# A graph network's gated projection: bias sums, third parts and chunk weights moved around the seam of its first two quarters

## The chip, the cores and the metric

The kernel runs on one core of a Trainium2 chip. A core has five engines that run at the same time, each with its own instruction stream: TensorE (PE, matrix products; the weight loads before them are shown as PEld), VectorE (DVE), ScalarE (ACT), GpSimd (POOL) and SyncE (SP, whose queue issues most of the DMAs). They wait for each other through semaphores. The metric is the time of one execution in microseconds (us), as the median of repeated runs. A profile is one further execution recorded by the chip's hardware profiler.

## The reference

x holds 1024 nodes with 512 features, in 16 graphs of 64 nodes; every graph has a condition of 256 rows. The sizes that matter: D = 512, H = 8 heads of DH = 64, L = 4 layers, and a gated projection whose inner width is 4D = 2048.

```python
h = (x - mu) * rsqrt(var + EPS) * bn_w + bn_b
h = gcn(h, src, dst, gcn_in_w, gcn_in_b)            # sum over 16384 edges
for i in range(L):
    h = h + attn(ln(h, ln2_w[i], ln2_b[i]), cond, Wq[i], Wk[i], Wv[i], Wo[i])
    u = ln(h, ln3_w[i], ln3_b[i]) @ geglu_w[i] + geglu_b[i]      # 512 -> 4096
    val, gate = split(u, 2, axis=-1)                             # 2 x 2048
    f = val * gelu(gate)
    h = h + f @ ffo_w[i] + ffo_b[i]                              # 2048 -> 512
h = gcn(h, src, dst, gcn_out_w, gcn_out_b)
return x + (h + x_in)
```

The change lies in the last three lines of the loop, and in the last of the attention's stages before them.

## The kernel before

**Stages of a layer.** The attention goes over eight pairs of graphs, g = 0 to 7, 128 rows of h each (the tiles called hall in the profile). The gated projection has a value and a gate side of 2048 columns; it is worked in quarters of 512 columns, and a quarter in four pieces of 128, so sixteen pieces in all. The output product follows in units.

All large products are done with seven instead of eight block products (Strassen's way, in Winograd's form), so sums of blocks have to be made first: `sums_of_b` and `sums_of_a` (L229 to L242), `Chunk.sums` (L1086 to L1094).

**Quarter 0** is the class `Quad`, four of them, with plain f32 products (L297). Their first two products (`first`, `second`, tile ga) are interleaved with the end of the attention's last pair. There, the softmax of pair 7 is scaled (pr, L852, on VectorE), turned by TensorE (tr_pr), copied out of PSUM by VectorE and ScalarE in turn (pT, L884 and L886), and multiplied by the values (po, L870). `rest(fill)` does the other five products (tiles gb, gc, gd) with VectorE's additions between them and the activation by ScalarE (L1002). It calls `fill()` five times, and each call drives one step of a generator that prepares the next quarters, `all_parts`.

**Quarters 1 to 3** are twelve objects of class `Chunk`. Their f32 products are replaced by three fp32r products of parts: a high, a low and a third part of each operand. Of the right side (the LayerNorm's output, the same for all chunks) six of seven operands are split so, in the order `SPLIT = (0, 5, 6, 4, 1, 3)`: ScalarE makes the high part and a multiple of it, VectorE makes the third part (gr, L1044, `begin_right`) and the low part (gl, L1052, `finish_right`). Both are two VectorE operations of 128x512 for each operand, one for each half k. The left side is a chunk's weights. They are loaded by four DMAs on SP into gxa and gxb (L1084), summed by GpSimd (L1094) and split by `split_left`: high part by ScalarE (gha, ghb, L1057), low part by VectorE (gla, glb, L1058), third part by GpSimd (gsa, gsb, L1061).

A chunk is a flow of six steps, `steps`. `scale(i)` does the first two products of operand i and has ScalarE multiply the bank by 1 + TINY (L1124), `scale_onto(i)` lets VectorE do it and add a term (L1128), and `end(i)` adds the third product. The flows of two chunks overlap: while one starts, the one before it ends. Its results fT are stored to a DRAM buffer (f_dram, L1194) and fetched again by the output units (fr). These need parts as well: ah_f, al_f and as_f of fr (L314 to L317) and bh, bl and bs of the output weights wff (`split_w`, L1229 to L1236). Some of the latter are made early by the generator `output.ahead()`, in steps placed by the table `splits`.

**What sets the order.** A scheduler orders instructions by costs and due times, but whatever is wrapped in `pin` keeps the order of the program text on its engine; nearly all of the seam is pinned. `issue_after` and `waiting_for` add dependencies by hand. Tiles come from pools of fixed size, so a tile that is asked for waits until an earlier one of its ring has been read: `t512` (ten of 128x512), `slot` (36 of 128x1024) and `acc_tile`. SP issues DMAs in the order of the text, and a DMA that waits holds those behind it.

**The places that are touched** (lines of the kernel before): the loop over pairs, where `ln3_sums(nc.gpsimd, nb)` sums the LayerNorm's blocks on GpSimd; `add_bias` (L1532), which adds the output's bias to a tile of hall on GpSimd, eight times behind the last LayerNorm sums; `all_parts`; the loop over the quads, with the loads and splits of the first two chunks in it; the loop over the chunks; and the table `beside` of work for the next layer during the output units.

Of the kernel before, what the change touches and what calls it, by code (L numbers as in the profile page):

```python
# [11 lines left out]
F32R = mybir.dt.float32r  # L12
# [13 lines left out]
def gnn_kernel(  # L26
# [1010 lines left out]
    def begin_right(name, x, h, s):  # L1037

        nc.scalar.mul(h.bitcast(F32R), x, INWARD / TINY)
        for k in range(2):  # L1040
# [3 lines left out]
            pin(nc.vector.scalar_tensor_tensor(s.bitcast(F32R)[:, k, :], x[:, k, :], 1.0 / TINY,  # L1044
                                               more, OP.mult, OP.subtract))

    def finish_right(name, x, h):

        low = slot(name)
        for k in range(2):  # L1050
            yield low
            pin(nc.vector.scalar_tensor_tensor(low.bitcast(F32R)[:, k, :], x[:, k, :], 1.0 / TINY,  # L1052
                                               h[:, k, :], OP.mult, OP.subtract))
# [390 lines left out]
    for l in range(L):  # L1444
# [80 lines left out]
        def ln3_sums(t, nb):  # L1525

            c0 = nb % 4 * P
            of = [ln3T[i][k][:, :, c0:c0 + P] for k in range(2) for i in range(2)]
            return sums_of_b(t, *of, *(x[:, :, c0:c0 + P] for x in ln3S), nc.gpsimd)
# [36 lines left out]
        for g in range(NG - 1):  # L1566
            if g == NG - 2:
                take_ln3()
                raw = load_geglu(l, 0)
            probs = scores(l, g, qT, kTs.pop(g))  # L1570
            for end in ends:
                end()
            if g == NG - 2:
                with waiting_for(scores.last, mybir.EngineType.Pool):
                    left = geglu_weights(l, 0, *raw)
            if not g:
                with waiting_for(scores.last, mybir.EngineType.Pool):
                    wo7 = wo_sums(wo)
            if g in (1, 2):
                fetch_x(2 * l + g - 1)  # L1580
            k = keys(l, g + 1, wk, 1 if l == 0 and g == 0 else 0)
            for i, u in enumerate(k):
                u.begin()
                if i > 1:
                    k[i - 2].end()
            k[-2].end()
            v = values(l, g + 1, wv)
            oTs.append(mix(l, g, probs, vs.pop(g), (k[-1].end, nothing, v[0].begin)))
            if g == NG - 2:
                ln3_norm(g - 2, g - 1, behind=mix.last)  # L1590
            if g in (1, 2):
                base_of(2 * l + g - 1)
            if l == 0:
                fetch_cond(g + 3)
            if g % 2:
                blocks = pair_sums(l, g - 1, oTs)
                oTs.clear()
            with tc.issue_after(pair_sums.last.ins) if g % 2 else nullcontext():
                split_cond(l, g + 2)
            if l:  # L1600
                load_cond(l, g + 3)
            v[1].begin()
            v[0].end()
            v[2].begin()
            v[1].end()
            if g % 2:
                pair = attn_out_pair(g - 1, *blocks, wo7, bank(f"oab_{l}_{g}"), bank(f"ocd_{l}_{g}"),
                                     pin)
                next(pair)
                if g > 1:  # L1610
                    moments_into(mv_kept[:, 2 * (g - 3):2 * (g - 1)], [h[g - 3], h[g - 2]],
                                 f"ln3_{l}_{g - 3}")
            if g == NG - 2:
                for nb in range(4):
                    ln3_turn(nb, each=pin)
            v[3].begin()
            if g % 2:
                next(pair)
            v[2].end()
            ends = [v[3].end]  # L1620
            if g % 2:
                next(pair)
                ends.insert(0, lambda pair=pair: next(pair, None))
                if g == NG - 3:
                    scale_kept()
            if g == NG - 2:
                for nb in range(4, 6):
                    ln3_turn(nb, each=pin)
                for nb in (g - 2, g - 1):
                    ln3_sums(nc.gpsimd, nb)  # L1630
            if l == 0 and g + 3 < NG:
                turn_cond(g + 3, each=pin)
        oT, = oTs
# [17 lines left out]
        ln3_turn(g, (1, 1))  # L1651
        summed = ln3_sums(nc.vector, g)
        with tc.issue_after(summed.ins):
            for nb in range(NB):
                add_bias(nb)
        quads[2].second()
        quads[3].second()
# [10 lines left out]
        def finish_rights(*of):  # L1668
            for i in of:
                x, high, mid = begun[i]  # L1670
                flow = finish_right(f"gl_{l}_{i}", x, high)
                Chunk.rights[i] = high, next(flow), mid
                yield
                for _ in flow:
                    yield

        def all_parts():
            for i in SPLIT:
                yield from begin_right(f"gt_{l}_{i}", *begun[i])
                yield from finish_rights(i)  # L1680

        parts = all_parts()
        next(parts)
# [18 lines left out]

        for c, q in enumerate(quads):
            q.rest(fill)
            if c == 1:
                load()
                sum_chunk(0)
            if c == 2:
                split(0, False)
                split(0, True)  # L1710
        for _ in parts:
            pass
        load()
        sum_chunk(1)
        output = Output(l)
        ahead = output.ahead()
        fetches = [(R - 2, 0), (R - 2, 3), (R - 1, 1), (R - 1, 3)]
        splits = {(R - 2, 1): 3, (R - 2, 2): 2, (R - 1, 0): 3, (R - 1, 1): 2}
        before = None
        for r in range(1, R):  # L1720
            f = Gated(l, r)
            for c in range(KC):
                if (r, c) in fetches:
                    output.fetch_w(fetches.index((r, c)))
                if (r, c) == (R - 1, KC - 2):
                    output.fetch(0)
                chunk = ready.pop(0)
                flow = chunk.steps(lambda: sum_chunk(1))
                chunk.f = f
                next(flow)  # L1730
                split(0, False)
                load()
                for step in range(3):
                    if before:
                        next(before, None)
                    next(flow)
                    if step < splits.get((r, c), 0):
                        next(ahead)
                split(0, True)
                before = flow  # L1740
        output.split(0)
        output.fetch(1)
        for _ in range(3):
            next(before, None)

# [4 lines left out]
        if last:  # L1750
            hs_out.extend(RowsInTurn(f"hs_{n}_out") for n in ("high", "low"))

            def begin_last():
                for nb in (0, 1, 4, 5):
                    into_parts(nb)

            def fetch_counts():
                nonlocal again, dinv_row
                again, dinv_row = load_counts()

            def fetch_last():
                nonlocal w_out
                w_out = out_weights(nc.gpsimd, L, 0, load_w(gcn_out_w, "w_out"))

            beside = {8: begin_last, 9: fetch_counts, 13: fetch_last}
        else:
            half = [0, 1, 4, 5], [2, 3, 6, 7]
            wk, wv = [[], [], []], [[], [], []]

            def fetch_next():  # L1770
                nonlocal raw_wk
                raw_wk = load_w(Wk[l + 1], f"wk_{l + 1}")
                load_cond(l + 1, 0)

            def fetch_values():
                nonlocal raw_wv
                raw_wv = load_w(Wv[l + 1], f"wv_{l + 1}")

            def split_of(to, raw, name, i):
                for part, t in zip(to, right_parts(raw[i:i + 1], f"{name}_{l + 1}_{i}")):  # L1780
                    part.extend(t)

            def norm_first():
                take_moments(l + 1, half[0], 2)
                ready_first(l + 1, half[0])

            def fetch_more():
                nonlocal wq, ffb
                wq = load_w(Wq[l + 1], f"wq_{l + 1}")
                ffb = load_row(ffo_b, (l + 1) * D, f"ffb_{l + 1}")  # L1790
                load_cond(l + 1, 1)

            beside = {8: lambda: (fetch_next(), take_moments(l + 1, half[0], 0, 2)),
                      9: lambda: split_of(wk, raw_wk, "wk", 0),
                      10: lambda: split_of(wk, raw_wk, "wk", 1),
                      11: lambda: (norm_first(), fetch_values()),
                      12: lambda: split_cond(l + 1, 0),
                      13: lambda: split_of(wv, raw_wv, "wv", 0),
                      14: fetch_more}
        with in_order(mybir.EngineType.DVE):  # L1800
            for n in range(2 * UNITS):
                output.fetch(n + 2)
# [143 lines left out]
```

## Time and profile before

| | |
|---|---|
| time, median of 3 runs | 2390.27 us (2388.44 to 2392.40) |
| profiled execution | 2390.05 us, span 2388.3 us |
| mean granted TensorE clock | 0.994 |
| TensorE busy | 2324.4 us, 97% |
| VectorE busy | 1585.6 us, 66% |
| ScalarE busy | 1082.1 us, 45% |
| GpSimd busy | 794.7 us, 33% |

The span runs from the first to the last instruction; the execution's own time has what lies around it too. A row of the timeline gives the start (us from the span's start), the time that the group took, the engine, the line, the operation, what it writes and reads, its shape and count, and in brackets the idle time of its engine before it and who ended that. A row of busy time by windows gives the length, each engine's busy time and instruction count (PE, PEld, VectorE, ScalarE, GpSimd), the granted clock, the DMA share and GB/s. The four layers look alike; the rows that are shown are of the third (l = 2), which begins its gated projection at 1497.80.

### The profile page before, as it was taken

The numbers are of one execution on the slowest core, as the hardware profiler recorded it, in microseconds if no ns is written. First come the engines' busy times: TensorE is split into PE (matmuls) and PEld (weight loads), VectorE is DVE, ScalarE is ACT, GpSimd is POOL, SyncE is SP. The second block draws the span as 40 slices with busy tenths as digits, with TensorE's granted clock in tenths as the row PEclk, the third lists the DMA queues.
The fourth block names the chain that finished last, engine by engine and source line by source line (L and its number), as shares of the span: only waits on it lengthen the run. The fifth ranks groups of instructions, "written<-read, shape, count | busy, mean of one in ns | idle before, by whom it ended". The sixth has DMA issues, their size and how long they took to land. (4 is left out here: it accounts for less than half of the span.)

```text
span 2388.3 us, 33592 instructions
## 1 busy us (share of the span) xinstructions
PE 2324.4 (97%) x12272; PEld 1722.9 (72%) x12272; DVE 1585.6 (66%) x3024; ACT 1082.1 (45%) x2099; POOL 794.7 (33%) x731
## 2 busy tenths in 40 slices
PE   8999999899999999899999999989999999989999
PEld 5668886477867887477876888467786888557787
DVE  9874546777964445777984454867886554777864
ACT  7444454455344444454344444445334444445420
POOL 1142223563023224465022323466022224356211
PEclk9999999999999999999999999999999999999999
DMA  6052220235412110234522201134432111033550
GB/s 202 18 156 72 71 67 1 81 116 173 147 63 66 41 33 21 71 100 124 187 71 67 67 19 36 40 97 129 163 124 67 49 37 36 19 90 113 176 194 36
DMA packets 161068, 205.42 MB, mean 86 GB/s; under 512 B 11304, under 2 KB 101744, under 8 KB 160896
## 3 DMA queue, kind: packets, MB, share of 16 engines
q1 hardware_dynamic: 158800, 197.77, 26.0%
q0 software_dynamic: 1376, 4.30, 0.5%
q8 instruction: 102, 1.67, 0.3%
q10 hardware_dynamic: 720, 1.11, 0.1%
q14 instruction: 70, 0.57, 0.1%
HBM read 152.80 MB, written 50.34 MB: 85 GB/s over the span
## 5 line engine op out<-in xcount | busy, mean ns | idle before, releaser
L320 POOL TENSOR_TENSOR as_c<-ah_c,al_c 128x512 fp32r<-128x512 f32 x128 | 195.3, 1556 | 416.8 <-PE fy L1255 242.1
L1110 PE MATMUL g<-gr,gsa 128*128 128x512 f32 x384 | 142.0, 452 | 35.7 <-ACT g L1124 35.7
L377 ACT ACTIVATE v<-v 128x512 f32<-128x512 f32 x127 | 74.1, 583 | 220.5 <-PE v L366 218.4
L1061 POOL TENSOR_TENSOR gsa<-gha,gla 128x512 fp32r<-128x512 f32 x96 | 127.4, 1349 | 99.4 <-DVE gla L1058 99.4
L1255 PE MATMUL fx<-bs_wff,as_f 128*128 128x512 f32 x512 | 158.2, 390 | 2.0 <-DVE as_f L317 2.0
L1255 PE MATMUL fy<-bh_wff,ah_f 128*128 128x512 f32 x512 | 159.3, 392 | 0.0
L1255 PE MATMUL fy<-bl_wff,al_f 128*128 128x512 f32 x512 | 157.7, 389 | 0.0
L1124 ACT ACTIVATE g<-g 128x512 f32<-128x512 f32 x192 | 110.3, 581 | 99.3 <-PE g L1110 97.2
L314 ACT ACTIVATE ah_f<-fr 128x1024 fp32r<-128x1024 f32 x64 | 67.5, 1060 | 174.9 <-PE fy L1255 116.3
L366 PE MATMUL v<-bh_wv,ah_c 128*128 128x512 f32 x508 | 145.9, 409 | 0.0
L366 PE MATMUL v<-bs_wv,as_c 128*128 128x512 f32 x508 | 143.4, 404 | 0.0
L847 ACT ACTIVATE pr<-sc,nmax 128x256 f32<-128x256 f32 x256 | 118.3, 475 | 52.8 <-DVE nmax L842 52.1
L377 ACT ACTIVATE k<-k 128x512 f32<-128x512 f32 x125 | 72.7, 585 | 147.4 <-PE k L366 147.4
L366 PE MATMUL v<-bl_wv,al_c 128*128 128x512 f32 x508 | 136.4, 390 | 0.0
L366 PE MATMUL k<-ah_c,bh_wk 128*128 128x512 f32 x500 | 134.6, 391 | 0.0
L366 PE MATMUL k<-al_c,bl_wk 128*128 128x512 f32 x500 | 134.0, 390 | 0.0
L366 PE MATMUL k<-as_c,bs_wk 128*128 128x512 f32 x500 | 132.1, 395 | 0.0
L1137 ACT ACTIVATE g<-g,gcols 128x512 f32<-128x512 f32 x96 | 67.5, 704 | 132.4 <-DVE g L1145 129.9
L1110 PEld LDWEIGHTS g<-gr,gsa 128*128 128x128 f32 x384 | 72.4, 194 | 76.1 <-issue 61.8
L1110 PE MATMUL g<-gr,gha 128*128 128x512 f32 x384 | 121.0, 396 | 0.0
L1110 PE MATMUL g<-gl,gla 128*128 128x512 f32 x384 | 118.8, 390 | 0.0
L382 DVE COPY kT<-k 128x512 f32<-128x512 f32 x54 | 37.4, 692 | 118.4 <-PE k L366 118.4
(351 smaller groups left out, 5632.2 us busy)
## 6 DMA issues: line engine op xcount, KB each, us to landing
f_dram<-fT SPq DMA_DIRECT2D x128, 256.0 KB, 2.6
fr<-f_dram SPq DMA_DIRECT2D x64, 512.0 KB, 4.8
ct<-cond_dram SPq DMA_DIRECT2D x48, 512.0 KB, 4.4
wff<-in_L_gnn_ffo_w_dram SPq DMA_DIRECT2D x32, 512.0 KB, 4.8
gxb<-in_L_gnn_geglu_w_dram SPq DMA_DIRECT2D x96, 128.0 KB, 2.7
gxa<-in_L_gnn_geglu_w_dram SPq DMA_DIRECT2D x96, 128.0 KB, 2.8
cond<-in_L_gnn_cond_dram SPq DMA_DIRECT2D x32, 256.0 KB, 3.6
cond_dram<-ct SPq DMA_DIRECT2D x16, 512.0 KB, 4.0
```

Of the source, the lines that this page charges most:

```text
L314: nc.scalar.mul(twelve_bits(h), x, INWARD * TINY)
L320: nc.gpsimd.tensor_tensor(twelve_bits(s)[:, k, :], h[:, k, :], l[:, k, :], OP.subtract)
L366: pin(nc.tensor.matmul(self.bank, twelve_bits(left[k // 2])[:, k % 2, self.c * P:(self.c + 1) * P], twelve_bits(right[k // 2])[:, k % 2, : ...
L377: nc.scalar.mul(self.bank, self.bank, 1.0 + TINY)
L382: nc.vector.tensor_copy(self.to(), self.bank)
L847: nc.scalar.activation(pr3[:, a, :], ps3[:, a, :], AF.Exp, bias=nmax[:, a:a + 1], accum_out=tot[:, a:a + 1])
L1061: pin(nc.gpsimd.tensor_tensor(s_at, h_at, l_at, OP.subtract))
L1110: pin(nc.tensor.matmul(to, self.part(i, which)[:, k, :], self.rights[i][which].bitcast(F32R)[:, k, :], start=start and k == 0, stop=stop a ...
L1124: pin(nc.scalar.mul(to, to, 1.0 + TINY))
L1137: pin(nc.scalar.activation(to, of, AF.Gelu, bias=gcols[:, cg:cg + 1]))
L1255: pin(nc.tensor.matmul(to, twelve_bits(left[which][0])[:, k, b * P:(b + 1) * P], twelve_bits(right[which])[:, k, :], start=u == 0 and whic ...
```

## The change

- Six of the eight bias additions go to the stage of pair g = 6, right behind GpSimd's LayerNorm sums there. Two stay behind the last sums.
- The last three of the six right operands, 4, 1 and 3, get their parts from a new function `right_with_pool`: VectorE makes the low part alone, and GpSimd makes the third part from it by a subtraction. ScalarE makes the same number of results as before.
- All the parts are finished after quad 2, not after quad 3, and ahead of the splits of chunk 0.
- Chunk 0's weights are loaded after quad 0 instead of inside the step after quad 1, chunk 1's after quad 2 instead of after quad 3. In program order, chunk 1's loads then come before quad 3's store.
- In the chunks, the early parts of the output weights come all ahead of the chunk's three steps, not one with each step.
- The first output unit's split and the fetch of the second unit go from behind the loop into the last chunk; one fetch of output weights goes behind the loop.
- Beside the output units, two steps for the next layer change places.

```diff
+    def right_with_pool(name, x, h, s):
+
+        low = slot(name)
+        nc.scalar.mul(h.bitcast(F32R), x, INWARD / TINY)
+        more = [t512(f"{name}_{k}") for k in range(2)]
+        for k in range(2):
+            nc.scalar.mul(more[k], h[:, k, :], TINY)
+            yield low
+            pin(nc.vector.scalar_tensor_tensor(low.bitcast(F32R)[:, k, :], x[:, k, :], 1.0 / TINY,
+                                               h[:, k, :], OP.mult, OP.subtract))
+            pin(nc.gpsimd.tensor_tensor(s.bitcast(F32R)[:, k, :], low[:, k, :], more[k],
+                                        OP.subtract))
...
                 for nb in (g - 2, g - 1):
                     ln3_sums(nc.gpsimd, nb)
+                for nb in range(g):
+                    pin(add_bias(nb))
...
         with tc.issue_after(summed.ins):
-            for nb in range(NB):
+            for nb in (g - 1, g):
                 add_bias(nb)
...
         def all_parts():
-            for i in SPLIT:
+            for i in SPLIT[:3]:
                 yield from begin_right(f"gt_{l}_{i}", *begun[i])
                 yield from finish_rights(i)
+            for i in SPLIT[3:]:
+                x, high, mid = begun[i]
+                flow = right_with_pool(f"gl_{l}_{i}", x, high, mid)
+                Chunk.rights[i] = high, next(flow), mid
+                yield
+                for _ in flow:
+                    yield
...
         for c, q in enumerate(quads):
             q.rest(fill)
+            if c == 0:
+                load()
             if c == 1:
-                load()
                 sum_chunk(0)
             if c == 2:
+                for _ in parts:
+                    pass
                 split(0, False)
                 split(0, True)
-        for _ in parts:
-            pass
-        load()
+                load()
         sum_chunk(1)
...
-        fetches = [(R - 2, 0), (R - 2, 3), (R - 1, 1), (R - 1, 3)]
+        fetches = [(R - 2, 0), (R - 2, 3), (R - 1, 1)]
...
                 split(0, False)
                 load()
+                for _ in range(splits.get((r, c), 0)):
+                    next(ahead)
+                if (r, c) == (R - 1, KC - 1):
+                    output.split(0)
+                    output.fetch(1)
                 for step in range(3):
                     if before:
                         next(before, None)
                     next(flow)
-                    if step < splits.get((r, c), 0):
-                        next(ahead)
                 split(0, True)
                 before = flow
-        output.split(0)
-        output.fetch(1)
+        output.fetch_w(3)
...
-                      13: lambda: split_of(wv, raw_wv, "wv", 0),
-                      14: fetch_more}
+                      13: fetch_more,
+                      14: lambda: split_of(wv, raw_wv, "wv", 0)}
```

## The prediction

> **What bounds the kernel now.** I read the page first (busy time of each engine), then the granted clock and the busy times by stage, then the groups of TensorE instructions for the seam, and last the rows of each engine around every wait that these named.
>
> ```profile
> PE 2324.4 (97%) x12272; PEld 1722.9 (72%) x12272; DVE 1585.6 (66%) x3024; ACT 1082.1 (45%) x2099; POOL 794.7 (33%) x731
> ```
>
> TensorE is busy for 97% of the span, so an edit counts by what it does to PE's idle time. By stages of the third layer, whose windows are the first part of quarter 0 (with the end of attention in it), its interleaved rest, the chunks, and the output units:
>
> ```profile
> 1497.80:1519.80 22.00, 22.00 (x129) 11.79 (x128) 15.00 (x53) 5.96 (x12) 1.10 (x3) 1.00 0.00 1
> 1519.80:1555.70 35.90, 34.33 (x82) 14.76 (x80) 31.26 (x45) 17.90 (x25) 20.66 (x16) 1.00 0.23 73
> 1555.70:1688.50 132.80, 123.19 (x481) 90.99 (x480) 95.54 (x136) 67.40 (x111) 75.98 (x77) 0.97 0.38 114
> 1688.50:1777.00 88.50, 88.01 (x387) 72.38 (x386) 81.76 (x106) 27.32 (x27) 8.32 (x4) 1.00 0.50 172
> ```
>
> The columns are the length, then busy time of PE, PEld, DVE, ACT, POOL, the granted clock, the DMA share and GB/s. PE is idle for 0 us in the first window, 1.57 in the second, 9.6 in the third. The third is the only one with a clock under 1.00. Next, the rows that hold these 9.6 and 1.57 (last brackets: idle time before, and who ended it):
>
> ```profile
> 1552.56 1.98 PE L297 MATMUL gc<-ln3S,wgate 128*128 128x512 f32 x4 [1.57 <-DVE gu L1012]
> 1555.69 1.02 PE L1110 MATMUL g<-gr,gha 128*128 128x512 f32 x2
> ...
> 1560.34 0.61 PE L1110 MATMUL g<-gl,gla 128*128 128x512 f32 x2
> 1567.57 1.19 PE L1110 MATMUL g<-gr,gsa 128*128 128x512 f32 x2 [6.62 <-ACT g L1124]
> 1568.56 1.05 PE L1110 MATMUL g<-gr,ghb 128*128 128x512 f32 x2
> ...
> 1625.31 0.70 PE L1110 MATMUL g<-gr,gsa 128*128 128x512 f32 x2 [0.75 <-ACT g L1124]
> ...
> 1635.91 0.70 PE L1110 MATMUL g<-gr,gsa 128*128 128x512 f32 x2 [0.40 <-ACT g L1124]
> ```
>
> The big one is at the seam, inside the first chunk. Pairs of matmuls that follow it take 1.05 instead of 0.61 for five pairs, about 2.1 us more. Its chain, backwards:
>
> ```profile
> 1565.41 1.06 ACT L1057 ACTIVATE gha<-gxa 128x1024 fp32r<-128x1024 f32 x1 [6.69 <-POOL gxa L1094]
> 1563.17 0.72 POOL L1094 TENSOR_TENSOR gxa<-gxa,gxb 128x256 f32<-128x256 f32 x1 [8.47 <-DMA gxa<-in_L_gnn_geglu_w_dram]
> 1559.69 2.18 SPq L1084 DMA_DIRECT2D gxa<-in_L_gnn_geglu_w_dram  x4
> ```
>
> ScalarE's split of chunk 1's weights stands in program order ahead of the scaling that PE waits for; it waits for GpSimd's sums, these for weights that SP issues only after quarter 0's last store.
>
> **The change, part by part.** All costs are for one layer; there are four alike.
>
> *Bias adds.* Six of the eight additions to hall leave the point after the last LayerNorm sums and follow GpSimd's sums of the second-last pair, with nothing to wait for. GpSimd's and VectorE's rows there:
>
> ```profile
> 1496.29 0.72 POOL L234 TENSOR_TENSOR ln3S<-ln3T,ln3S 128x256 f32<-128x256 f32 x1
> 1497.09 0.73 POOL L235 TENSOR_TENSOR ln3S<-ln3T,ln3S 128x256 f32<-128x256 f32 x1
> 1517.03 0.72 POOL L235 TENSOR_TENSOR ln3S<-ln3T,ln3S 128x256 f32<-128x256 f32 x1 [19.21 <-DVE ln3S L234]
> ...
> 1520.12 12.21 POOL L1532 TENSOR_TENSOR hall<-hall,ffb 128x512 f32<-128x512 f32 x8
> ...
> 1617.10 2.54 POOL L1061 TENSOR_TENSOR gsa<-gha,gla 128x512 fp32r<-128x512 f32 x2 [1.35 <-DVE gla L1058]
> ```
>
> ```profile
> 1496.37 1.60 DVE L852 TENSOR_SCALAR pr<-pr,inv 128x256 f32<-128x256 f32 x2
> 1498.08 1.14 DVE L852 TENSOR_SCALAR pr<-pr,inv 128x256 f32<-128x256 f32 x4
> 1499.33 0.62 DVE L852 TENSOR_SCALAR pr<-pr,inv 128x256 f32<-128x256 f32 x2
> 1503.53 1.28 DVE L884 COPY pT<-tr_pr 128x512 f32<-128x512 f32 x2
> ```
>
> GpSimd idles from 1497.82 to 1517.03, so the six fit. But they start with VectorE's softmax scaling (pr) of the last pair. The two pr operations that met GpSimd's sums took 0.80 each; the six that met none took about 0.30. A pr that meets one waits it out: the second ends at 1497.97, 0.15 after the sum it met (1497.82). An add takes about 1.27 free, an estimate from the two equally large subtractions of 2.54 at 1617.10, so with alternation six pr's take 1.4 each instead of 0.3: the last ends near 1506.1 instead of 1499.95. VectorE's 3.6 us between that and the pT copies stays, and so the copies start near 1509.7. PE's order here:
>
> ```profile
> 1501.23 1.91 PE L201 MATMUL tr_pr<-ident,pr 128*128 128x128 f32 x16
> 1502.98 1.88 PE L297 MATMUL ga<-ln3T,wval 128*128 128x512 f32 x4
> 1504.79 2.08 PE L870 MATMUL po<-pT,v 128*64 128x64 f32 x64
> ```
>
> po needs the first of the copies (0.68) and follows four ga matmuls that no longer cover anything: it starts near 1510.5, +5.7. Bounds: 0, if adds and pr don't meet, and 6 x 1.27 = 7.6, if VectorE gets nothing until all are through; plus 2.1 above, if the slow clock follows as after the seam. I take 5.7, since both pr rows that met GpSimd show the wait. What the adds leave behind (12.21 at 1520.12 becomes about 3) is worth nothing: PE has no idle time there.
>
> *Third parts on GpSimd, and all parts done before quad 3.* VectorE loses six operations of 128x512, GpSimd gains six. ScalarE has equal counts. The flush after quad 3 moves to before it, ahead of the first half's split:
>
> ```profile
> 1547.80 0.68 DVE L1052 SCALAR_TENSOR_TENSOR gl<-ln3S,gr 128x512 fp32r<-128x512 f32 x1
> 1548.40 1.22 DVE L1058 SCALAR_TENSOR_TENSOR gla<-gha,gxa 128x1024 fp32r<-128x1024 f32 x1
> 1549.53 0.69 DVE L1058 SCALAR_TENSOR_TENSOR glb<-ghb,gxb 128x512 fp32r<-128x512 f32 x1
> 1550.13 0.69 DVE L1012 TENSOR_TENSOR gu<-gb,gs 128x512 f32<-128x512 f32 x1
> 1550.73 1.17 DVE L1052 SCALAR_TENSOR_TENSOR gl<-ln3S,gr 128x512 fp32r<-128x512 f32 x1
> 1551.82 0.68 DVE L1012 TENSOR_TENSOR gu<-gc,gu 128x512 f32<-128x512 f32 x1
> ```
>
> ```profile
> 1549.76 3.26 POOL L1061 TENSOR_TENSOR gsa<-gha,gla 128x512 fp32r<-128x512 f32 x2 [10.03 <-DVE gla L1058]
> 1552.99 1.72 POOL L1061 TENSOR_TENSOR gsb<-ghb,glb 128x512 fp32r<-128x512 f32 x1
> ```
>
> Beside GpSimd's gsa the same VectorE operation took 1.17 instead of 0.68, and a GpSimd one 1.63 to 1.72; operations that read PSUM (gu) did not slow. Between quad 2's fT and quad 3's second gu, on which gc waits, stand four SBUF operations now and six then (four low parts, gla, glb). Free, gu would end at 1552.50 + 2 x 0.60 - 0.50 (no blocked gl) = 1553.2. GpSimd has four third parts and gsa to do in that stretch; if four of the six each wait for one, at a pitch of 1.72 instead of 0.60, gu ends near 1557.7. So gc waits 1.57 + 5.1 = 6.7, between bounds of +0.7 and +5.1. I take the upper: work is queued on both engines all through the stretch. The added waits (glb for GpSimd's first subtraction, quad 2's g0 for its third, chunk 2's second load for the fourth) are met earlier than this one. As to SP, the loads there queue behind the delayed fourth, and only chunk 2 needs them, some 10 us later.
>
> *Loads ahead.* Chunk 0's DMAs go after quad 0 and chunk 1's after quad 2, so ahead of quad 3's store. Issue to landing was 1559.69 to 1563.17, so issued near 1549 they land near 1553. Then GpSimd is the later one: seven operations (four third parts, two gsa, one gsb) at 1.63 from 1548.5 end near 1560.0, three sums to 1562.2 (2.24 from 1563.17 to 1565.41), gha to 1563.3 or so. PE starts the chunk at 1555.69 + 5.1 = 1560.8 and reaches the stalled matmul 5.26 later (10 pairs, 1555.69 to 1560.95), at 1566.0: the 6.62 is gone. It ran at 1567.57 before, hence -1.6. The 2.1 of slow clock is left in both: after 6.62 us here, after 6.7 there. With gu free (+0.7) PE is there at 1561.65 and GpSimd is through before: -5.9, or -8.0 with the slow clock gone.
>
> *Parts of the output weights.* All of a chunk's share now precedes its three steps. ScalarE's bh comes ahead of a copy with slack of a microsecond or more. VectorE's two come right behind gla, where it idled; the second then meets GpSimd's gsa:
>
> ```profile
> 1628.01 2.92 POOL L1061 TENSOR_TENSOR gsa<-gha,gla 128x512 fp32r<-128x512 f32 x2 [1.16 <-DVE gla L1058]
> ```
>
> ```profile
> 1618.31 0.75 DVE L1175 SCALAR_TENSOR_TENSOR fT<-g,gcols,g 128x512 f32<-128x512 f32 x1 [1.28 <-ACT g L1137]
> ...
> 1630.36 1.13 DVE L1236 SCALAR_TENSOR_TENSOR bs_wff<-bh_wff,bl_wff 128x512 fp32r<-128x512 f32 x1
> ```
>
> Two operations free need 1.20 of the idle 1.28; but gsa runs from 1617.10 to 1619.64 (row above), and blocked as bs was (1.13), the second ends a gsa half later, and fT, g1, its gate and the next chunk's scaling slip. By that count 0.75 becomes 1.05 and 0.40 becomes 1.0; the same pair follows in the last quarter: +1.8. Unblocked, these four waits go: -1.9. I take +1.8, as bs in this very place was blocked.
>
> *Last chunk.* The first output unit's split moves ahead of its steps, where ScalarE idles:
>
> ```profile
> 1685.55 0.70 PE L1110 MATMUL g<-gr,gsb 128*128 128x512 f32 x2 [0.35 <-DVE g L1128]
> 1686.66 0.73 PE L1110 MATMUL g<-gr,gsb 128*128 128x512 f32 x2 [0.40 <-DVE g L1128]
> ```
>
> Both waits are for VectorE behind al_f and as_f, and go: -0.75 (0 at worst). The later fourth fetch of output weights and the exchange of two steps beside the output units lie under 88.01 busy of 88.50 and cost nothing; without that cover a late fetch would show as a wait of its landing time.
>
> *Sum, by the values taken:* 5.7 - 1.6 + 1.8 - 0.75 = +5.15 a layer, +20.6 over four. The profiled execution took 2390.05 (span 2388.3), 0.2 under the median, so about 2410.
>
> **The page's rules.** By the Trainium skill ("SBUF — State Buffer", section "Who interferes with whom") a VectorE instruction with two SBUF inputs excludes a reading GpSimd instruction, while one with at most one SBUF input, outside the two-port modes, does not contend. The 1.17 agrees; whether pr falls under the second half no run shows beyond its 0.80 beside GpSimd. By that half the adds are free: the rival below, 2388. By "TensorE: Matmul & The Clock Gate" (Part 1, "What's actually happening") an idle window of about 3.4 us halves the clock; the pairs at 1.05 agree. If it also saw attention's broken wait as idle, 2.1 a layer more would give 2419.
>
> **Rivals.** (1) *The seam opens and the engines don't collide:* the change does what its moves suggest. Third parts find GpSimd between VectorE's operations, adds are free. 4 x (-0.75 - 1.9 - 5.9) = -34, or -43 with the clock: 2347 to 2356; with half of the collisions at the seam (-3.8) and at the weights (0), 4 x -4.5 = -18: 2372. For it: the 6.62 with its slow clock is by far the largest wait. Against: 1.17 for 0.68. It decides if gu ends before 1555. (2) *Adds free, rest as summed:* 4 x (-1.6 + 1.8 - 0.75) = -2: 2388. Against: 0.80 twice. (3) *Adds cost, the seam opens:* 4 x (5.7 - 0.75 - 1.9 - 5.9) = -11: 2379, or 2394 with the weights blocked. (4) *The slow clock comes on top in attention:* 2419, to 2428 with the adds at 7.6.
>
> **How the numbers follow.** Forecast, 2402 to 2416: 0.47. Rival 1: 0.19 (a third of it at half strength). Rival 2: 0.10. Rival 3: 0.09. Rival 4: 0.15. Faster or slower is told from 0.2%, 4.8 us. Faster: 0.19, two thirds of rival 3 and a third of rival 2, 0.28. Same: the rest of rival 2, 0.07. Slower: 0.65. The range leaves out rival 1 at full strength and the far end of rival 4: 2370 to 2426.
>
> **What would show it.** The six adds stand right behind GpSimd's sums near 1497.8; pr rows of 1.3 instead of 0.3; po with idle time before it, copies near 1509.7. If pr stays at 0.3, this step is wrong and the time falls by 20 us. At the seam: gc's wait over 6 and the chunk's 6.62 gone; if gc waits under 3, rival 1 or 3 holds. Waits at the second quarter's chunks of about 1.0, and none before the last two gsb.

## The result, and the profile after

The changed kernel takes 2406.84 us (median of 4 runs, 2404.11 to 2412.01) where the kernel before took 2390.66 (4 runs). The ratio is 1.0071, with a 95% interval of 1.0051 to 1.0090: slower by 16.2 us, or about 4.0 for each of the four layers. The profiled execution has a span of 2404.2 against 2388.3.

The page's busy times of the changed kernel:

```profile
PE 2328.3 (97%) x12272; PEld 1722.1 (72%) x12272; DVE 1617.4 (67%) x3000; ACT 1081.0 (45%) x2099; POOL 834.5 (35%) x755
```

VectorE has 24 instructions fewer (six a layer) and is yet 31.8 us longer busy (1617.4 against 1585.6). It has less to compute: an instruction that is held off counts as busy, as its rows below show. The same stages of the third layer as in the prediction (first part of quarter 0, its interleaved rest, chunks, output units):

```profile
1506.31:1533.44 27.13, 22.95 (x129) 11.93 (x128) 20.64 (x53) 5.96 (x12) 8.75 (x9) 1.00 0.05 15
1533.44:1576.07 42.63, 35.88 (x82) 15.62 (x80) 34.08 (x45) 18.39 (x26) 22.74 (x20) 0.92 0.19 59
1576.07:1701.14 125.07, 120.76 (x482) 89.57 (x481) 95.08 (x129) 67.25 (x111) 75.81 (x74) 1.00 0.40 122
1701.14:1788.76 87.62, 87.62 (x387) 72.41 (x386) 80.86 (x105) 26.88 (x27) 8.84 (x4) 1.00 0.50 168
```

Against before these are +5.1, +6.7, -7.7 and -0.9 us, +3.3 in all. That is the cheapest of the four layers: by the starts of the stages, the first, second and fourth come to +4.2, +4.5 and +4.1 (the rest of quarter 0 is up to 0.9 longer there, the second keeps a wait of 0.60 in its second chunk, and the fourth's output units gain nothing). The clock below 1.00 has moved from the chunks (0.97) to the rest of quarter 0 (0.92). TensorE's waits behind these sums, from its timeline:

```profile
1511.62 0.44 PE L201 MATMUL tr_pr<-ident,pr 128*128 128x128 f32 x2 [0.63 <-DVE pr L852]
1512.99 0.41 PE L201 MATMUL tr_pr<-ident,pr 128*128 128x128 f32 x2 [0.93 <-DVE pr L852]
1514.17 0.44 PE L201 MATMUL tr_pr<-ident,pr 128*128 128x128 f32 x2 [0.77 <-DVE pr L852]
...
1516.25 0.33 PE L870 MATMUL po<-pT,v 128*64 128x64 f32 x2
1518.44 2.08 PE L870 MATMUL po<-pT,v 128*64 128x64 f32 x62 [1.85 <-DVE pT L884]
...
1571.26 3.65 PE L297 MATMUL gc<-ln3S,wgate 128*128 128x512 f32 x4 [6.75 <-DVE gu L1012]
...
1637.14 0.70 PE L1123 MATMUL g<-gr,gsa 128*128 128x512 f32 x2 [1.03 <-ACT g L1137]
1648.32 0.70 PE L1123 MATMUL g<-gr,gsa 128*128 128x512 f32 x2 [0.98 <-ACT g L1137]
...
1669.46 0.70 PE L1123 MATMUL g<-gr,gsa 128*128 128x512 f32 x2 [1.03 <-ACT g L1137]
1680.60 0.70 PE L1123 MATMUL g<-gr,gsa 128*128 128x512 f32 x2 [0.94 <-ACT g L1137]
1699.26 0.73 PE L1123 MATMUL g<-gr,gsb 128*128 128x512 f32 x2 [0.33 <-DVE g L1141]
```

The first chunk, where the 6.62 stood, has no wait any more. In its place gc waits 6.75 us some 5 us earlier, and the four gc matmuls behind it take 3.65 instead of 1.98. VectorE and GpSimd at both places, from their timelines:

```profile
1506.57 4.99 DVE L852 TENSOR_SCALAR pr<-pr,inv 128x256 f32<-128x256 f32 x4
1511.67 2.44 DVE L852 TENSOR_SCALAR pr<-pr,inv 128x256 f32<-128x256 f32 x2
1517.70 1.28 DVE L884 COPY pT<-tr_pr 128x512 f32<-128x512 f32 x2
...
1562.52 3.42 DVE L1055 SCALAR_TENSOR_TENSOR gl<-ln3S,gr 128x512 fp32r<-128x512 f32 x2
1565.86 2.28 DVE L1071 SCALAR_TENSOR_TENSOR gla<-gha,gxa 128x1024 fp32r<-128x1024 f32 x1
1568.06 1.74 DVE L1071 SCALAR_TENSOR_TENSOR glb<-ghb,gxb 128x512 fp32r<-128x512 f32 x1
1569.73 0.68 DVE L1012 TENSOR_TENSOR gu<-gb,gs 128x512 f32<-128x512 f32 x1
```

```profile
1506.27 7.69 POOL L1545 TENSOR_TENSOR hall<-hall,ffb 128x512 f32<-128x512 f32 x6
...
1562.17 7.09 POOL L1057 TENSOR_TENSOR gr<-gl,gl 128x512 fp32r<-128x512 f32 x4 [1.51 <-ACT gha L1070]
1569.22 2.93 POOL L1074 TENSOR_TENSOR gsa<-gha,gla 128x512 fp32r<-128x512 f32 x2
```

Six adds take 1.28 each, undisturbed, and the six pr operations beside them 1.22 to 1.25 each instead of 0.3. Before quad 3, four VectorE operations and the four third parts take turns: 1.71, 1.71, 2.28 and 1.74 us on VectorE, where the same operations took 0.68, 0.68, 1.22 and 0.69 before.

### The profile page after: what moved, and what is told of

Same layout as the page of the kernel before. It is cut to its first block, busy times and chain, and to the rows that moved or that the text cites. A ratio compares the mean times of both kernels' runs of the same rounds, so it can differ in the third digit from the quotient of the medians.

```text
span 2404.2 us, 33599 instructions
## 1 busy us (share of the span) xinstructions
PE 2328.3 (97%) x12272; PEld 1722.1 (72%) x12272; DVE 1617.4 (67%) x3000; ACT 1081.0 (45%) x2099; POOL 834.5 (35%) x755
## 3 DMA queue, kind: packets, MB, share of 16 engines
q8 instruction: 102, 1.67, 0.3%
## 5 line engine op out<-in xcount | busy, mean ns | idle before, releaser
L1074 POOL TENSOR_TENSOR gsa<-gha,gla 128x512 fp32r<-128x512 f32 x96 | 136.6, 1443 | 71.1 <-DVE gla L1071 45.5
L919 POOL TENSOR_TENSOR os<-oT 128x256 f32<-128x256 f32 x12 | 8.8, 734 | 318.8 <-DVE oT L893 291.5
```

Of the source, the lines that this page charges most:

```text
L1074: pin(nc.gpsimd.tensor_tensor(s_at, h_at, l_at, OP.subtract))
```

## The experiments

Each was compared with the kernel before on the same chip; sums by layer are of the third layer.

**Only the adds put back.** The changed kernel, less this edit:

```diff
-                for nb in range(g):
-                    pin(add_bias(nb))
...
-            for nb in (g - 1, g):
+            for nb in range(NB):
                 add_bias(nb)
```

> The changed kernel with all eight bias adds put back behind the last LayerNorm sums. Theory (the six adds on GpSimd hold up VectorE's scaling of the last pair's probabilities, one add per operation): the first part of quarter 0 falls from 27.14 us a layer to the 22.01 of before, the waits in front of tr_pr and po are gone, and the time falls by 4 x 5.1 = 20.5 to about 2386. Rival (the longer attention stage only moves a wait that would come at the seam anyway): the wait of gc at the seam grows by as much, and the time stays above 2400.

Measured: 2387.42 us (ratio 0.9992, 0.9983 to 1.0002: no difference from before that can be told). The adds alone made the change slow; all else together came out even.

```profile
1497.68:1519.69 22.01, 22.01 (x129) 11.79 (x128) 15.01 (x53) 5.96 (x12) 1.13 (x3) 1.00 0.07 19
1519.69:1563.08 43.39, 36.63 (x82) 15.80 (x80) 34.91 (x45) 18.79 (x26) 32.86 (x26) 0.92 0.19 58
```

The first part is back at 22.01, PE without idle time. In the rest of quarter 0 gc waits 6.76, as in the changed kernel (6.75), so the wait at the seam does not depend on the adds, and the rival falls.

**Only the adds moved.** The kernel before with the edit that the last run took away.

> The kernel before with only the six bias adds moved behind GpSimd's LayerNorm sums of pair 6. Theory: the same 5.1 us a layer, all else as before, so 2390.5 + 20.5 = 2411; the seam's 6.62 stays. Rival (the price comes from the whole of the change, for instance because the parts of the right side also run late): under 2400.

Measured: 2416.87 us (1.0110, 1.0093 to 1.0126), 27.4 slower than the kernel before (2389.45): by the stage it is 6.7 a layer (28.71 against 22.00), not 5.1. The waits are the same to 0.01 us (0.64, 0.93, 0.77, 1.86). The rest is clock:

```profile
1510.92:1539.63 28.71, 24.51 (x129) 13.24 (x128) 20.67 (x53) 5.96 (x12) 8.77 (x9) 0.94 0.00 1
```

PE is 1.56 us longer busy in this stage than in the changed kernel's (24.51 against 22.95) with the same matmuls, at a clock of 0.94: here the slow clock comes behind the broken wait and slows po and what follows. In the changed kernel's first two layers it came earlier and fell into the wait itself, where it cost nothing:

```profile
399.89 3.04 PE L297 MATMUL ga<-ln3T,wval 128*128 128x512 f32 x4
402.86 0.48 PE L870 MATMUL po<-pT,v 128*64 128x64 f32 x2
403.88 2.08 PE L870 MATMUL po<-pT,v 128*64 128x64 f32 x62 [0.54 <-DVE pT L884]
```

The four ga matmuls take 3.04 instead of 1.88, and po waits 0.54 instead of 1.85; the stage is 27.13 long either way.

**Three adds instead of six.**

```diff
-                for nb in range(g):
+                for nb in range(3):
                     pin(add_bias(nb))
...
-            for nb in (g - 1, g):
+            for nb in range(3, NB):
                 add_bias(nb)
```

> The kernel before with three of the bias adds moved behind GpSimd's LayerNorm sums of pair 6, five left in place. Theory (one probability scaling waits out one add): three scalings take 1.23 instead of 0.3, VectorE's pT copies come 2.8 later instead of 5.6, the wait of po after a slack of about 0.6 makes 2.2 a layer and no slow clock follows: 2390 + 9 = 2399. Rival (GpSimd's adds hold VectorE off until all are through, or the price is the slow clock that follows a wait of a certain length): no proportion to the count, 2390 or over 2410.

Measured: 2402.87 us (1.0051, 1.0036 to 1.0066), 12.0 slower or 3.0 a layer, where 2.2 was expected.

```profile
1503.24 3.98 DVE L852 TENSOR_SCALAR pr<-pr,inv 128x256 f32<-128x256 f32 x4
1507.33 0.62 DVE L852 TENSOR_SCALAR pr<-pr,inv 128x256 f32<-128x256 f32 x2
```

```profile
1510.11 0.33 PE L870 MATMUL po<-pT,v 128*64 128x64 f32 x2
1512.27 3.56 PE L870 MATMUL po<-pT,v 128*64 128x64 f32 x62 [1.83 <-DVE pT L884]
```

Three of the six scalings are held (3.98 for four of which one is free, then 0.31 each), so one operation pays one add; the rival that VectorE gets nothing until GpSimd is through falls. The layer's wait is 1.83, but po then runs at the slow clock here too (3.56 instead of 2.08). So the rival's second half, the clock, is real: in three layers of four the stage is 25.8 long (22.01 + 1.83 + about 2.0), in the first 24.3.

**The adds behind the scaling.**

```diff
         probs = scores(l, g, qT, kTs.pop(g))
+        with waiting_for(scores.last, mybir.EngineType.Pool):
+            for nb in range(g - 1):
+                pin(add_bias(nb))
...
-            for nb in range(NB):
+            for nb in (g - 1, g):
                 add_bias(nb)
```

> The kernel before with the six bias adds behind the last scaling of pair 7 on VectorE instead of ahead of it. Theory (an add holds off any VectorE operation whose operands all lie in SBUF): the scalings take 0.3 again, but nine operations on 128x1 with two SBUF inputs in the LayerNorm chain that follows meet the adds, up to six of them wait 1.2 each, the pT copies come up to 7 late, and the time is 2395 to 2420. Rival (so small an operation doesn't wait for GpSimd): no price, 2390.

Measured: 2411.59 us (1.0082, 1.0065 to 1.0099). The scalings are free again (0.3), but VectorE's LayerNorm chain behind them, which stands ahead of the pT copies, is not:

```profile
1514.14 0.65 DVE L156 SCALAR_TENSOR_TENSOR a_ln<-y_ln,v_ln 128x1 f32<-128x1 f32 x1
1514.82 1.19 DVE L158 TENSOR_TENSOR b_ln<-a_ln,y_ln 128x1 f32<-128x1 f32 x1
1516.05 1.19 DVE L160 SCALAR_TENSOR_TENSOR y_ln<-b_ln,y_ln 128x1 f32<-128x1 f32 x1
1517.27 1.19 DVE L156 SCALAR_TENSOR_TENSOR a_ln<-y_ln,v_ln 128x1 f32<-128x1 f32 x1
1518.49 1.18 DVE L158 TENSOR_TENSOR b_ln<-a_ln,y_ln 128x1 f32<-128x1 f32 x1
1519.70 0.16 DVE L160 SCALAR_TENSOR_TENSOR y_ln<-b_ln,y_ln 128x1 f32<-128x1 f32 x1
```

An operation on one column takes 1.19 instead of 0.16 while an add runs. Two neighbours in the chain that don't read two tensors of SBUF (L151, L153 on 128x1, at 1513.76 and 1513.95) stay at 0.15, though GpSimd is at its adds from 1512.27 on. Nor is the statistics operation of 128x512 on hall held (L168, 0.69 at 1512.82). po waits 3.73 in the end, and runs at the slow clock behind that (3.68 instead of 2.08).

**Only the loads moved.** The kernel before with the loads ahead; parts, adds and places as they were:

```diff
             q.rest(fill)
+            if c == 0:
+                load()
             if c == 1:
-                load()
                 sum_chunk(0)
             if c == 2:
                 split(0, False)
                 split(0, True)
+                load()
         for _ in parts:
             pass
-        load()
```

> The kernel before with only the loads of the first two chunks' weights moved (after quad 0 and after quad 2); the parts stay on VectorE and are finished after quad 3 as before, the adds stay. Theory (the 6.62 at the seam hangs on the issue of chunk 1's loads behind quad 3's store): GpSimd's sums of chunk 1 start right behind its gsb near 1555 instead of 1563.2, the 6.62 and its slow clock (2.1) go, gc's 1.57 stays: 8.7 a layer, about 2356. Rival (the loads wait for a free tile, or land no earlier, so that the sums still come near 1563): no change, 2390.

Measured: 2361.19 us (0.9879, 0.9862 to 0.9895), 7.1 a layer faster.

```profile
1505.38:1541.23 35.85, 34.29 (x81) 14.82 (x80) 31.36 (x45) 17.90 (x25) 22.16 (x17) 1.00 0.22 69
1541.23:1666.91 125.68, 121.56 (x482) 89.39 (x481) 95.79 (x136) 67.22 (x111) 76.43 (x77) 1.00 0.40 119
```

```profile
1538.53 1.71 POOL L1061 TENSOR_TENSOR gsb<-ghb,glb 128x512 fp32r<-128x512 f32 x1
1540.20 1.18 POOL L1094 TENSOR_TENSOR gxa<-gxa,gxb 128x256 f32<-128x256 f32 x1
```

The sums for chunk 1 start right behind gsb, the 6.62 is gone and the clock is 1.00. A new wait of 1.05 stands at the second chunk, which is most of what is missing between 7.1 and 8.7; the other half microsecond is TensorE's busy time in the chunks, which fell by 1.6 (123.19 to 121.56) where 2.1 was expected. The load order was worth more than the whole change cost.

**The third parts without GpSimd.** From the changed kernel with the adds back:

```diff
-        more = [t512(f"{name}_{k}") for k in range(2)]
         for k in range(2):
-            nc.scalar.mul(more[k], h[:, k, :], TINY)
+            nc.scalar.mul(s.bitcast(F32R)[:, k, :], h[:, k, :], TINY)
...
-            pin(nc.gpsimd.tensor_tensor(s.bitcast(F32R)[:, k, :], low[:, k, :], more[k],
-                                        OP.subtract))
```

> As adds_back, but without GpSimd's six subtractions for the third parts of operands 4, 1 and 3: ScalarE writes the multiple of the high part straight into the third part, so this kernel leaves out the low part's share in it; the order and count of VectorE's and ScalarE's instructions stay. Theory (collision of VectorE's and GpSimd's SBUF operations): gc waits 2 to 3 us instead of 6.75, without the slow clock behind it, so some 6 us a layer less than adds_back: about 2361. Rival (the wait comes from the order alone, from all parts being finished ahead of quad 3): gc waits over 5 and the time is that of adds_back, about 2386.

Measured: 2362.83 us (0.9881, 0.9864 to 0.9897), 24.6 less than adds_back.

```profile
1541.32 1.98 PE L297 MATMUL gc<-ln3S,wgate 128*128 128x512 f32 x4 [2.49 <-DVE gu L1012]
```

```profile
1536.84 1.29 DVE L1054 SCALAR_TENSOR_TENSOR gl<-ln3S,gr 128x512 fp32r<-128x512 f32 x2
1538.04 1.22 DVE L1068 SCALAR_TENSOR_TENSOR gla<-gha,gxa 128x1024 fp32r<-128x1024 f32 x1
1539.18 0.68 DVE L1068 SCALAR_TENSOR_TENSOR glb<-ghb,gxb 128x512 fp32r<-128x512 f32 x1
```

The same VectorE operations in the same order now take their free times, and gc waits 2.49 instead of 6.75, in all four layers. The order (all parts ahead of quad 3) accounts for 0.9 of the added 5.2, the meeting of the two engines for the other 4.3. The slow clock is not wholly gone, as the windows of the rest of quarter 0 in the second and third layer show; the third was the only layer without it:

```profile
960.69:999.17 38.48, 35.99 (x81) 15.48 (x80) 30.34 (x45) 18.57 (x26) 22.98 (x20) 0.96 0.22 66
1507.67:1544.45 36.78, 34.29 (x81) 14.87 (x80) 30.43 (x45) 18.56 (x26) 21.19 (x18) 1.00 0.22 68
```

**Only the places of the output weights' parts.**

```diff
                 load()
+                for _ in range(splits.get((r, c), 0)):
+                    next(ahead)
                 for step in range(3):
...
-                    if step < splits.get((r, c), 0):
-                        next(ahead)
```

> The kernel before with only the early parts of the output weights put ahead of a chunk's three steps. Theory (the last of them meets GpSimd's gsa and delays fT and the gate behind it): the four waits of 0.75, 0.40, 0.75 and 0.35 a layer become about 1.0 each, +1.8 a layer, 2397. Rival (they fill VectorE's idle time behind gla and the four waits go): 2381.

Measured: 2397.61 us (1.0026, 1.0016 to 1.0037), +6.7. The four waits are 1.02, 0.99, 1.02 and 0.95. VectorE beside GpSimd's gsa (1620.87, 3.37 for two instead of 2.54):

```profile
1620.71 0.68 DVE L1232 SCALAR_TENSOR_TENSOR bl_wff<-wff,bh_wff 128x512 fp32r<-128x512 f32 x1
1621.42 1.66 DVE L1236 SCALAR_TENSOR_TENSOR bs_wff<-bh_wff,bl_wff 128x512 fp32r<-128x512 f32 x1
```

**Only the last chunk's edits**, with the fetch behind the loop and the exchange beside the output units:

```diff
+                if (r, c) == (R - 1, KC - 1):
+                    output.split(0)
+                    output.fetch(1)
                 for step in range(3):
...
-        output.split(0)
-        output.fetch(1)
+        output.fetch_w(3)
...
-                      13: lambda: split_of(wv, raw_wv, "wv", 0),
-                      14: fetch_more}
+                      13: fetch_more,
+                      14: lambda: split_of(wv, raw_wv, "wv", 0)}
```

> The kernel before with only the first output unit's split and the second's fetch in the last chunk, the fourth fetch of output weights behind the loop, and the exchange of two steps beside the output units. Theory: the waits of 0.35 and 0.40 before the last two gsb go, and the output units take 0.8 less as in the changed kernel (their wait of 0.49 for as_f is gone): -1.5 a layer in three layers and -0.75 in the last, 2385. Rival (these two gains belong to the parts of the weights being early, not to this edit): 2390.

Measured: 2385.32 us (0.9976, 0.9965 to 0.9986), 5.6 faster. One of the two waits before the last gsb goes, the other stays at 0.34; the output units take 0.8 less in three layers of four. These rows make some 4 us of the 5.6 (4 x 0.4 and 3 x 0.8); the interval reaches from 3.3 to 8.4.

**Loads and last chunk together.** The two edits shown above, on the kernel before.

> The kernel before with the moved loads of the chunks' weights and with the edits of last_chunk; third parts on VectorE, adds and parts of the output weights where they were. Theory: the gains add up, loads_only's 2361.2 less 5 is about 2356. Rival (the freed seam shifts GpSimd's work onto the last chunk's VectorE operations): 2361 or more.

Measured: 2355.87 us (0.9852, 0.9837 to 0.9867). That is 35.0 faster, and the two gains make 28.3 + 5.6 = 33.9: they add up.

**Third parts on GpSimd where it idles.** On top of that, operand 6 (pool_one) or operands 6 and 4 (pool_two) go through `right_with_pool`, in their turn; the rest and the flush after quad 3 stay:

```diff
             for i in SPLIT:
-                yield from begin_right(f"gt_{l}_{i}", *begun[i])
-                yield from finish_rights(i)
+                if i not in (6,):
+                    yield from begin_right(f"gt_{l}_{i}", *begun[i])
+                    yield from finish_rights(i)
+                    continue
+                x, high, mid = begun[i]
+                flow = right_with_pool(f"gl_{l}_{i}", x, high, mid)
+                Chunk.rights[i] = high, next(flow), mid
+                yield
+                for _ in flow:
+                    yield
```

> loads_and_last with the third parts of one operand (6) on GpSimd, whose subtractions fall into its idle stretch before its first gsa; the parts are finished after quad 3 as before. Theory (what made the third parts dear was the crowd before quad 3, not the engine): VectorE is rid of two operations of 0.6, gc's 1.57 shrinks by up to 1.2, so 2351 to 2356. Rival (each subtraction costs VectorE as much as it saves, since the low parts wait for it): 2356 or up to 2361.

> As pool_one with two operands (6 and 4). Theory: gc's wait shrinks further, 2349 to 2355. Rival: the second operand's subtractions come beside the first gsa and GpSimd's sums, gc waits over 2, 2360 or more.

Measured: 2352.81 us (0.9841, 0.9825 to 0.9857) and 2353.01 us (0.9841, 0.9824 to 0.9857).

```profile
1536.53 1.98 PE L297 MATMUL gc<-ln3S,wgate 128*128 128x512 f32 x4 [1.56 <-DVE gu L1012]
```

Both stay in the expected times, but not by the expected way: gc's wait is not shorter (1.56 in pool_one, 1.82 in pool_two), and the rest of quarter 0 is longer (36.23 and 36.50 instead of 35.85). What went in the third layer is the second chunk's 1.05; in the second layer 0.75 and 1.27 of it are left. The subtractions of operand 6 run at 1.27 and 1.28, undisturbed, in GpSimd's idle stretch. Whether these two beat loads_and_last is open: the intervals overlap. All three beat the kernel before by about 1.5%, and the changed one by more.

## Why the prediction was right

The forecast was 2410, in a range of 2402 to 2416 for its own case; 2406.84 was measured. The two engines' meeting, on which it rested at all three places, is what the runs show. Of the 20.6 that it summed up, 16.2 came; by terms, in the third layer (5.15 forecast, 3.3 measured):

*Bias adds, taken as 5.7 a layer: right in mechanism, 0.6 too dear.* The copies start 5.66 later against the start of the stage (11.39 in 1517.70, 5.73 in 1503.53), where the sum had 6.2 (1509.7 against 1503.53). It took 1.4 for each scaling, the add's 1.27 and the 0.15 by which one had ended behind a sum; beside a queue of adds a scaling takes 1.22 to 1.25, no more than an add. The 0.5 that po had in hand before is in the sum, and comes off again: 5.1. One reading was wrong and cost nothing: po's first two matmuls don't wait for VectorE's copies (they run at 1516.25), only the other 62 do. adds_back and adds_only show the edit's price with all else fixed, adds_three that it goes by one add per operation.

*Third parts, gc waits 6.7: right* (6.75). That four operations each wait for one is what VectorE's rows show, and no_pool_thirds takes away the cause. The slow clock moved with the wait, as the sum had it; it cost 1.67 on gc's four matmuls (3.65 against 1.98).

*Loads ahead, -1.6 together with it:* the first chunk's wait is gone, and the rest of quarter 0 and the chunks, less the two terms below, make -2.3 in the third layer (6.7 - 7.7 - 1.7 + 0.4). The waits are about as forecast: 5.2 more at gc and 6.6 less in the chunk are -1.4. The other 0.9 is TensorE's busy time (1.55 more in the rest of quarter 0, 2.43 less in the chunks), where the sum, with 2.1 of slow clock before and after, had none. loads_only shows that -7.1 was to be had without the crowd ahead of quad 3: rivals 1 and 3 named the right prize and missed what stood in its way.

*Parts of the output weights, +1.8: right* (1.73 in the changed kernel; alone 6.7 over four layers, 1.7 each).

*Last chunk, -0.75: half right.* One of the two waits stays (0.33), so -0.42. It was not behind al_f and as_f: in the changed kernel neither stands ahead of VectorE's scaling there, which starts at 1698.51, right as the product that TensorE does just before ends (1697.84 and 0.63). And a step costed at nothing was a missing term, the exchange of two steps beside the output units: -0.8 in three layers of four. "88.01 busy of 88.50" still held 0.49 of idle time, and behind it a pair took 0.73 instead of 0.62. Before, VectorE's four operations for the next layer's wv (1764.80 to 1769.60) stood ahead of the al_f and as_f that end this wait; in the changed kernel they come behind them, and the wait is gone. last_chunk shows the same gain without the rest of the change:

```profile
1772.13 0.73 PE L1255 MATMUL fx<-bs_wff,as_f 128*128 128x512 f32 x2 [0.49 <-DVE as_f L317]
```

*Rivals.* Rivals 1 and 3 fall with gc's 6.75, rival 2 (adds free) with adds_only. Rival 4 (the slow clock on top in attention) cost nothing in the changed kernel, where the clock fell in two layers, inside the wait; it came true in adds_only, adds_three and adds_late. Its far end, given as 2428, is 2426.6 by its own terms (20.6, 4 x 2.1 and 4 x 1.9 on 2390.05); nothing hangs on that. By the Trainium skill ("TensorE: Matmul & The Clock Gate", Part 1, "What's actually happening") an idle window of some 3.4 us is what halves the clock. In adds_three the longest stretch without a matmul was 1.83 us, and the clock fell: the measurement goes against that length. It falls there behind some 6 us in which only four full matmuls (1.88) and sixteen transposes ran. What decides in which layers it falls ahead of po and in which behind it, no run here settles.

## What to carry to other kernels

Before work goes to GpSimd, look at what VectorE does in the same microseconds. In this kernel each VectorE operation on two SBUF tensors, and each scaling of 128x256, paid up to a whole GpSimd instruction, however small it was itself; operations that read PSUM, and some on one SBUF tensor, paid nothing. An idle engine is not a free one. Count the price per VectorE operation held, not per GpSimd operation added, and follow it to the first thing TensorE waits for. When a seam stalls on a load, move the load alone first; here that alone was worth 28 us, and the work that was moved along with it ate it all.

## What was not expected of the hardware

VectorE operations on 128x1 were held as long as large ones: 1.19 us instead of 0.16 beside a 128x512 add on GpSimd. GpSimd's adds hardly noticed (7.38 for six there, 7.69 beside the scalings), while its subtractions beside VectorE's 128x512 operations went from 1.27 to 1.77 (7.09 for four). By the Trainium skill ("SBUF — State Buffer", "Who interferes with whom") an operation with two SBUF inputs contends, and a tensor-scalar one only in a two-port mode; the 1.19 agrees, and so do L151, L153 and L168, which read one and were not held; that pr (128x256) was held would fit that mode, which no run here shows.

The slow clock came behind shorter waits than expected: behind 1.83 us of po's in three layers of adds_three, and behind gc's 2.49 in three layers of four in no_pool_thirds, never behind gc's 1.57, nor behind its 1.82 in pool_two. In adds_three's first layer the same 1.83 has none behind it. So the length of the wait alone does not decide it; what stood before it differs (transposes before po, full matmuls before gc), but no run here shows that this is the reason.
